# A state space scan followed by linear attention on one core: the state sums ahead of the next C row on TensorE, and D's products of a new y bank one slot sooner

## The chip, the cores and the metric

The kernel runs on one core of a Trainium2 chip. That core has five engines, each of which works through its own instructions in order: TensorE (PE in the profile; its weight loads are listed apart as PEld), VectorE (DVE), ScalarE (ACT), GpSimd (POOL), and SyncE (SP), which issues most of the transfers. The metric is the device time of one execution in microseconds (us). Before the change it was 7783.22 us, the median of three runs (7782.59 to 7801.19).

## The reference

The input is x, 4 x 512 x 64 x 64, in f32. Two layers are added to it, each on a group normalisation of what it gets.

The first is a state space model (Mamba). The 512 channels, normalised per token, are cut into four chunks of 128; each is a sequence of 4096 tokens. Per chunk:

```python
xz = einsum('bld,ed->ble', x, in_proj_w); xi, z = split(xz, 2)    # 256 inner channels each
xc = silu(conv(xi) + conv_b)                                      # 4 taps along the sequence
dt, Bs, Cs = x_proj(xc)                                           # Bs, Cs: 16 states
dt = softplus(dt_proj(dt) + dt_proj_b)
def step(h, inp):                                                 # for every token in turn
    dA = exp(dt_t[:, :, None] * A)
    h = dA * h + (dt_t * x_t)[:, :, None] * B_t[:, None, :]
    y = einsum('bds,bs->bd', h, C_t)                              # sum over the 16 states
y = (y + xc * D_param) * silu(z)
out = einsum('bld,od->blo', y, out_proj_w)
```

A skip, another normalisation over the 512 channels and a 512 x 512 projection follow. The second layer is linear attention with 8 heads: relu of q and k, k'q summed over all 4096 tokens of a batch, and v times that sum, normalised, with an output projection.

## The kernel before

**Tiles and steps.** The 4096 tokens of a batch are cut into 8 tiles of 512. One step works on one batch, tile and chunk, so there are 4 x 8 x 4 = 128 steps, four to a tile. The 256 inner channels are two halves `e` of 128. Four states and 32 channels lie on the 128 partitions, so a half needs four passes `q` over its 16 states, and a pass has four blocks `j` of 32 channels. A step thus has 8 passes and the kernel 1024.

**Slots.** The work is put down by hand, in slots (`slot`, L832 ff.). A pass has two slots, a step 16, numbered 0 to 15; `fold_states` of the pass in slots 0 and 1 is called in slot 2, and so on. In a slot:

- VectorE does two scans (L846) of 512 tokens, one for each block: `h = dA * h + bx`. The decay dA comes from ScalarE (L820) into one of three PSUM banks, bx from GpSimd (L828) into one of three buffers, two slots ahead.
- After the first scan of an even slot (the second in slot 10), `product` for the pass before: VectorE multiplies the first 384 columns of its h by the C row (L866). GpSimd has multiplied the last 128 columns by a part of C that came by DMA (L858, the tail product).
- Directly behind it `fold_states` gives TensorE its share of that pass, in the order below.
- `after()` then gives out everything else that falls to this slot: projections of the steps to come, normalisations, the output projection of the step before, and, from three queues (`ahead`, `late`, `rest`), pieces of the work between tiles. `rest` holds the attention of the batch before.

**What TensorE does in `fold_states`.** Three things, in this order:

1. The C row of the next pass (`c_row`): one bf16 product with a 0/1 matrix that spreads four rows of C over 128 partitions, 384 columns, into the one bank of `ps_c`. It overwrites the C row that `product` has just read, so it waits for `product`.
2. If the pass is the first of a half (`q == 0`, called in slots 2 and 10), a new y bank is taken from `ps_y`, which has one, and the diagonal goes into it: `D * xc` as four 32 x 32 products side by side (`diagonal`; 8 records in the profile, as each f32 product shows as two). The old y must have left the bank: ScalarE copies it out in `take_y` (L885), which is put down in slots 0 and 8.
3. The sum: four products with `fold`, side by side, that add the four states on the partitions (8 records). They read h, so they wait for `product` and for GpSimd's tail product.

h has two buffers. The first scan of a pass writes the buffer of two passes earlier, and needs that pass's sum to be done. After the fourth pass of a half, y is complete, and `take_y`, the gate and the output projection follow.

**How much goes into a slot.** TensorE's other work is rationed by a credit, in products of 512 columns. `mm` adds up what is given (`work["mm"]`); a diagonal counts 1.0, a sum 1.0, a C row 0.19. At the end of `after()`:

```python
credit = min(credit + 3.5 - (work["mm"] - seen), 2.6)
...                                    # pieces of ahead, late and rest, while credit > 0
seen = work["mm"]
```

So what `fold_states` gives between two calls of `after()` is charged at the next. Pieces of `rest` are given out only while the credit allows.

**After the loop** come the attention of the last batch and the output of its last tile, some 425 us with no scans.

All TensorE instructions are recorded by `mm`, so they share line L129 in the profile; they are told apart by tile: `c_all<-parts,sel` is the C row, `y<-xz,dg` the diagonal, `y<-h,fold` the sum.

Of the kernel before, what the change touches and what calls it, by code (L numbers as in the profile page):

```python
# [8 lines left out]
F32 = mybir.dt.float32  # L9
# [5 lines left out]
P = 128  # L15
T = 512
# [8 lines left out]
def kernel(  # L25
# [29 lines left out]
    NH = DI // P  # L55
# [14 lines left out]
    ps_y = ctx.enter_context(tc.tile_pool(name="ps_y", bufs=1, space=bass.MemoryType.PSUM))  # L70
# [55 lines left out]
    def mm(out_, lhsT, rhs, abreast=1, **how):  # L126

        work["mm"] += (0.25 if rhs.dtype == BF16 else 1.0) * rhs.shape[-1] / T / abreast
        nc.tensor.matmul(out_, lhsT, rhs, **how)  # L129
# [3 lines left out]
    def diagonal(out_, w, rhs):  # L133

        for k in range(P // BLK):
            r = slice(k * BLK, (k + 1) * BLK)
            mm(out_[r, :], w[r, :], rhs[r, :], abreast=P // BLK, start=True, stop=False)
# [130 lines left out]
    dg = const.tile([P, NH, BLK], F32, tag="dg", name="dg")  # L268
# [512 lines left out]
    SLOTS = NH * NQ * JJ  # L781
    AWAY = (3, 10)

    def place(g):

        n, r = divmod(g, SLOTS)
        e, r = divmod(r, NQ * JJ)
        return n, e, *divmod(r, JJ)

    b_all, c_all, c_sb, dAs, bxs, hs, ys = {}, {}, {}, {}, {}, {}, {}  # L790
# [18 lines left out]
    def c_row(g):  # L809
        n, e, q, _ = place(g)  # L810
        got = ps_c.tile([P, CUT], F32, tag="c", name=f"c_all_{g}")
        mm(got, sel[:, q, :], fs[n]["parts"], start=True, stop=True)
        c_all[g // JJ] = got
# [18 lines left out]
    def slot(g, last, after):  # L832
        n, e, q, jj = place(g)
        b, t, c = steps[n]
        if g + 2 < last:
            drive(g + 2)
        if jj == 0:
            if g + 3 * JJ < last:
                b_row(g + 3 * JJ)
            hs[g // JJ] = wk.tile([P, NJ, T], F32, tag="h", name=f"h_{g}", bufs=2)  # L840
        elif g + 1 < last:
            c_tail(g + 1)
        h = hs[g // JJ]
        for i in range(2):
            j = jj * 2 + i
            nc.vector.tensor_tensor_scan(  # L846
                h[:, j, :], dAs.pop(2 * g + i), bxs[g][:, i, :],
                0.0 if t == 0 else st[:, c, e, q, j : j + 1], ALU.mult, ALU.add,
            )
            if 2 * g + i + LEAD < 2 * last:  # L850
                decay(2 * g + i + LEAD)
            if i == int(g % SLOTS == AWAY[1]) and jj == 0 and g:
                product(g - 1)
                fold_states(g - 1, last)
        del bxs[g]
        if jj == JJ - 1:
            nc.gpsimd.tensor_copy(st[:, c, e, q, :], h[:, :, T - 1])  # L857
            nc.gpsimd.tensor_tensor(  # L858
                h[:, :, CUT:], h[:, :, CUT:], bc(c_sb.pop(g // JJ), NJ), ALU.mult
            )  # L860
        after()
# [6 lines left out]
    def fold_states(g, last):  # L868

        n, e, q, _ = place(g)  # L870
        if g + 1 < last:
            c_row(g + 1)
        if q == 0:
            ys[n, e] = ps_y.tile([P, T], F32, tag="y", name=f"y_{n}_{e}")
            diagonal(ys[n, e], dg[:, e, :], fs[n]["xz"][:, 0, e, :])
        h = hs.pop(g // JJ)
        for j in range(NJ):
            mm(
                ys[n, e][j * BLK : (j + 1) * BLK, :], fold, h[:, j, :],
                start=False, stop=(q == NQ - 1), abreast=NJ,  # L880
            )


    def take_y(f, n, e):
        nc.scalar.copy(f["xz"][:, 0, e, :], ys.pop((n, e)))  # L885
# [273 lines left out]
    fs = [{} for _ in steps]  # L1159
# [54 lines left out]
    def one(queue, may=ANYWHERE):  # L1214

        while queue:
            if queue[0][1] not in (None, "wait", "more", "free") and queue[0][1] not in may:
                return False  # L1220
            queue[0][1] = next(queue[0][0], queue)
            if queue[0][1] is not queue:
                return queue[0][1] != "wait"
            queue.pop(0)
        return False
# [67 lines left out]
    with tc.manual_schedule():  # L1293
        credit, seen, mix, held[0], held_x[0] = 0.0, work["mm"], iter(()), 0, 0
        for n, (b, t, c) in enumerate(steps):
            f, nm = fs[n], names[n]
# [9 lines left out]
            for s in range(SLOTS):  # L1306
                def after():
# [62 lines left out]
                    if s - 1 in AWAY:  # L1370
                        for queue in (ahead, late, rest):
                            if queue and queue[0][1] == "free":
                                one(queue)
                    seen = work["mm"]

                slot(n * SLOTS + s, N * SLOTS, after)
            fs[n - 1].clear() if n else None
        product(N * SLOTS - 1)
        fold_states(N * SLOTS - 1, N * SLOTS)
        now[0] = None  # L1380
        for _, what in due:
# [61 lines left out]
```

## Time and profile before

| | us |
|---|---|
| median of three runs | 7783.22 |
| the profiled execution, its own time | 7786.57 |
| its span, first to last instruction | 7784.8 |
| loop of the 128 steps, within the span | 92.8 to 7359.3 |
| C rows (1024): busy, mean of one | 367.5, 0.359 |
| diagonals (2048 records): busy, mean of one record | 354.9, 0.770 |
| sums (8192 records): busy, mean of one record | 1266.5, 0.694 |
| scans (3584 with a state): busy, mean of one | 4354.7, 1.264 |
| products (1024): busy, mean of one | 1767.7, 1.726 |
| tail products on GpSimd (1024): mean of one | 1.271 |
| bx on GpSimd (2048): busy, mean of one | 4826.9, 2.369 |
| TensorE idle ahead of a C row, until the product's end | 1004.0 in 462 places |

The mean granted clock of TensorE is 0.906. In the profile, busy times of an engine are unions: records that run side by side, like the four products of a sum, count once, so the mean of one record is not a fourth of the time of a sum. A wait is given with the instruction that waited and the one that ended the wait; only the last of several is named. In a row of the timeline the first number is the start, the second the length, and the bracket holds the idle time before it and what ended it.

### The profile page before, as it was taken

To read this page: it belongs to the slowest core of one execution; us is meant where nothing else is said; L and a number is where in the kernel's file an instruction comes from. 1 tells how busy PE (TensorE), PEld (TensorE's weight loads), DVE (VectorE), ACT (ScalarE), POOL (GpSimd) and SP (SyncE) were. 2 spreads that over 40 slices of the span, in tenths; PEclk is the share of its full clock that TensorE was granted. 3 is DMA by queue.
4 is the path that set the end of the run, shared out by engine and by line. 5 is a ranking of instruction groups with operands and counts; after the bars stand their busy time and mean duration, and the time that the engine had idled before them with its cause. 6 is when DMAs were issued, how large, how long until landed. Compare 5 with 4: busy or idle time off the path is not lost.

```text
span 7784.8 us, 90406 instructions
## 1 busy us (share of the span) xinstructions
PE 6430.9 (83%) x24784; PEld 2088.4 (27%) x24784; DVE 6983.2 (90%) x5816; ACT 5442.9 (70%) x8288; POOL 6897.0 (89%) x4638
## 2 busy tenths in 40 slices
PE   5677777767789888988789888898788888899699
PEld 1111221112223222322222223332122222233144
DVE  6999999999999999999999999899999999999821
ACT  5677777777777777777777777777777777777521
POOL 5999999999999999999999999999999999999700
PEclk8788788888899999998898999999799999999799
DMA  6666666666666656676766666677666655677502
GB/s 176 169 168 170 154 158 153 163 161 169 172 181 162 155 161 163 184 194 172 174 163 175 172 159 159 162 190 193 161 168 162 164 148 153 164 197 191 135 33 92
DMA packets 829216, 1265.33 MB, mean 163 GB/s; under 512 B 184072, under 2 KB 317720, under 8 KB 816416
## 3 DMA queue, kind: packets, MB, share of 16 engines
q1 hardware_dynamic: 806352, 1225.99, 60.3%
q0 software_dynamic: 16368, 32.51, 2.4%
q8 instruction: 194, 3.18, 0.2%
q14 instruction: 318, 2.61, 0.1%
q10 hardware_dynamic: 5984, 1.06, 0.1%
HBM read 1052.25 MB, written 206.57 MB: 162 GB/s over the span
## 4 chain that ended last, share of the span: by engine, by line
DVE 36%; PE 33%; ACT 10%; issue 7%; DMA 6%; POOL 5%; SPq 2%; DVEq 0%; POOLq 0%; ACTq 0%
DVE h L846 23%; DVE h L866 11%; PE y L129 6%; PE pc L129 6%; PE pq L129 6%; POOL bx L828 4%; ACT dA L820 4%; PE pr L129 3%; PE po L129 3%; PE pp L129 2%; DMA d_all<-d_rows 2%; DMA c_sb<-c_rows 2%; DVE xn L439 2%; SPq L795 2%; PE c_all L129 1%
## 5 line engine op out<-in xcount | busy, mean ns | idle before, releaser
L828 POOL TENSOR_TENSOR bx<-d_all,b_all 128x1024 f32<-128x1024 f32 x2048 | 4826.9, 2369 | 204.4 <-DVE h L846 187.5
L846 DVE TENSOR_TENSOR_SCAN h<-dA,st,bx 128x512 f32<-128x512 f32 x3584 | 4354.7, 1264 | 305.6 <-PE y L129 111.8
L820 ACT ACTIVATE dA<-d_all,a_t 128x512 f32<-128x512 f32 x4096 | 2759.0, 688 | 1499.1 <-DVE h L846 1445.2
L866 DVE TENSOR_TENSOR h<-h,c_all 128x1536 f32<-128x1536 f32 x1024 | 1767.7, 1726 | 0.1
L858 POOL TENSOR_TENSOR h<-h,c_sb 128x512 f32<-128x512 f32 x1024 | 1301.4, 1271 | 97.2 <-DMA c_sb<-c_rows 11.5
L129 PE MATMUL y<-h,fold 128*32 128x512 f32 x8192 | 1266.5, 694 | 51.6 <-POOL h L858 49.8
L129 PE MATMUL c_all<-parts,sel 128*128 128x384 bf16 x1024 | 367.5, 359 | 1005.5 <-DVE h L866 1004.0
L129 PE MATMUL pc<-xn,w_cv 128*128 128x512 f32 x2048 | 1047.6, 645 | 127.8 <-DVE xn L439 68.1
L129 PE MATMUL pq<-w_qk,xa 128*128 128x512 f32 x2048 | 965.9, 607 | 2.5 <-ACT xa L397 2.5
L846 DVE TENSOR_TENSOR_SCAN h<-dA,bx 128x512 f32<-128x512 f32 x512 | 590.0, 1202 | 39.1 <-POOL bx L828 15.5
L129 PEld LDWEIGHTS pc<-xn,w_cv 128*128 128x128 f32 x2048 | 389.9, 201 | 742.2 <-issue 413.5
L129 PEld LDWEIGHTS <-sel 128*128 128x128 bf16 x1216 | 120.6, 99 | 1655.6 <-DVE h L866 1443.1
L129 PEld LDWEIGHTS pq<-w_qk,xa 128*128 128x128 f32 x2048 | 394.1, 195 | 446.5 <-issue 429.1
L129 PE MATMUL pp<-xn,w_pr 128*128 128x512 f32 x1024 | 478.1, 596 | 0.0
L129 PE MATMUL pr<-xb,m 128*128 128x512 f32 x1024 | 475.6, 602 | 2.5 <-ACT res L1126 1.6
L129 PE MATMUL y<-xz,dg 32*32 32x512 f32 x2048 | 354.9, 770 | 0.0
L129 PEld LDWEIGHTS y<-h,fold 128*32 128x32 f32 x8192 | 170.4, 114 | 641.8 <-issue 393.4
L888 POOL TENSOR_TENSOR xz<-xz 128x512 f32<-128x512 f32 x256 | 325.7, 1272 | 12.1 <-ACT xz L885 9.7
L731 POOL TENSOR_TENSOR dt<-dt,xz 128x1024 f32<-128x1024 f32 x127 | 300.1, 2363 | 1.9 <-ACT dt L723 1.9
L129 PE MATMUL pd<-xz,w_xp 128*128 128x512 f32 x512 | 291.0, 696 | 0.0
L129 PE MATMUL pz<-xn,w_z 128*128 128x512 f32 x512 | 270.7, 621 | 7.8 <-ACT xz L710 6.3
L857 POOL COPY st<-h 128x4 f32<-128x4 f32 x1024 | 210.3, 205 | 59.0 <-DVE h L846 54.4
(223 smaller groups left out, 5911.7 us busy)
## 6 DMA issues: line engine op xcount, KB each, us to landing
d_all<-d_rows SPq DMA_DIRECT2D x2040, 256.0 KB, 4.3
b_all<-b_rows SPq DMA_DIRECT2D x4096, 64.0 KB, 2.4
d_rows<-dt SPq DMA_DIRECT2D x254, 512.0 KB, 2.7
c_sb<-c_rows SPq DMA_DIRECT2D x4096, 16.0 KB, 3.5
xn<-in_x_dram SPq DMA_DIRECT2D x32, 1024.0 KB, 8.0
x<-xr SPq DMA_DIRECT2D x32, 1024.0 KB, 4.4
xa<-x SPq DMA_DIRECT2D x32, 1024.0 KB, 5.7
xb<-x SPq DMA_DIRECT2D x32, 1024.0 KB, 5.8
```

Source lines behind the costliest of these rows:

```text
L129: nc.tensor.matmul(out_, lhsT, rhs, **how)
L439: nc.vector.tensor_tensor(v, v, bc(m, NC), op)
L731: nc.gpsimd.tensor_tensor(f["both"][:, 1], f["both"][:, 0], f["xz"][:, 0], ALU.mult)
L795: nc.sync.dma_start(dst[k * BLK : (k + 1) * BLK, :], rows_[q * KS + k, :].partition_broadcast(BLK))
L820: nc.scalar.activation(dAs[k], fs[n]["d_all", e][:, 0, j, :], AF.Exp, scale=a_t[:, e, j, q : q + 1])
L828: nc.gpsimd.tensor_tensor(bxs[g], fs[n]["d_all", e][:, 1, jj * 2 : jj * 2 + 2, :], bc(b_all[g // JJ], 2), ALU.mult)
L846: nc.vector.tensor_tensor_scan(h[:, j, :], dAs.pop(2 * g + i), bxs[g][:, i, :], 0.0 if t == 0 else st[:, c, e, q, j : j + 1], ALU.mult, AL ...
L857: nc.gpsimd.tensor_copy(st[:, c, e, q, :], h[:, :, T - 1])
L858: nc.gpsimd.tensor_tensor(h[:, :, CUT:], h[:, :, CUT:], bc(c_sb.pop(g // JJ), NJ), ALU.mult)
L866: nc.vector.tensor_tensor(own, own, bc(c_all.pop(g // JJ), NJ), ALU.mult)
L888: nc.gpsimd.tensor_tensor(f["xz"][:, 1, e, :], f["xz"][:, 1, e, :], f["xz"][:, 0, e, :], ALU.mult)
```

## The change

`fold_states` gives the sum first and the C row of the next pass behind it. Taking a new y bank and its diagonal become a function of their own, `begin_y`, called at the end of `after()` in slots 1 and 9: behind everything else of that slot on TensorE and just before `seen` is set. Before, the same happened in slots 2 and 10, between the C row and the sum.

```diff
     def fold_states(g, last):
 
         n, e, q, _ = place(g)
-        if g + 1 < last:
-            c_row(g + 1)
-        if q == 0:
-            ys[n, e] = ps_y.tile([P, T], F32, tag="y", name=f"y_{n}_{e}")
-            diagonal(ys[n, e], dg[:, e, :], fs[n]["xz"][:, 0, e, :])
         h = hs.pop(g // JJ)
         for j in range(NJ):
             mm(
                 ys[n, e][j * BLK : (j + 1) * BLK, :], fold, h[:, j, :],
                 start=False, stop=(q == NQ - 1), abreast=NJ,
             )
-
+        if g + 1 < last:
+            c_row(g + 1)
+
+
+    def begin_y(n, e):
+        ys[n, e] = ps_y.tile([P, T], F32, tag="y", name=f"y_{n}_{e}")
+        diagonal(ys[n, e], dg[:, e, :], fs[n]["xz"][:, 0, e, :])
...
                         for queue in (ahead, late, rest):
                             if queue and queue[0][1] == "free":
                                 one(queue)
+                    if s % (SLOTS // NH) == 1:
+                        begin_y(n, s // (SLOTS // NH))
                     seen = work["mm"]
```

## The prediction

> **What bounds the kernel now.** I read the busy times, the waits of VectorE, the chain, a table of stretches, and one piece of the timeline. The words pass, sum, C row and diagonal are those of the section on the kernel.
>
> ```profile
> PE 6430.9 (83%) x24784; PEld 2088.4 (27%) x24784; DVE 6983.2 (90%) x5816; ACT 5442.9 (70%) x8288; POOL 6897.0 (89%) x4638
> ...
> DVE 36%; PE 33%; ACT 10%; issue 7%; DMA 6%; POOL 5%; SPq 2%; DVEq 0%; POOLq 0%; ACTq 0%
> ```
>
> No engine is alone in front. The stretches (length; busy time and instructions of PE, PEld, DVE, ACT, POOL; granted clock; DMA) show it for the loop and, in its order, for three tiles of the loop:
>
> ```profile
> 92.80:7359.30 7266.50, 5976.30 (x23246) 1882.48 (x23244) 6846.85 (x5514) 5329.61 (x8122) 6884.89 (x4617) 0.90 0.66 168
> ...
> 3235.70:3461.60 225.90, 202.58 (x737) 67.14 (x736) 212.46 (x165) 171.90 (x263) 215.21 (x144) 0.97 0.74 195
> 3461.60:3686.60 225.00, 188.00 (x690) 58.64 (x688) 211.60 (x164) 168.52 (x257) 214.17 (x144) 0.93 0.68 179
> 3686.60:3904.60 218.00, 161.47 (x603) 44.35 (x603) 209.34 (x181) 162.61 (x248) 214.89 (x150) 0.83 0.71 178
> ```
>
> In the loop VectorE is busy 94.2% and GpSimd 94.7%. VectorE's idle time there is 420 us, and its waits (waiter, releaser: us, times, longest) say what a reorder on TensorE can reach:
>
> ```profile
> DVE h L846 <- PE y L129: 126.7, 119, 3.7
> DVE h L846 <- ACT dA L820: 94.9, 101, 3.5
> ...
> DVE h L846 <- POOL bx L828: 51.2, 51, 5.5
> ```
>
> Counting scans in order (32 a step) puts the 126.7 us in slots 4 (14.3), 6 (18.3), 8 (25.1), 10 (17.8), 12 (43.5) and 14 (7.6): always the first scan of a pass, which needs the h buffer that the sum of two passes earlier frees. Slots 4 and 12, 57.8 us in 56 waits, follow the first pass of a y bank. One of them:
>
> ```profile
> 1394.78 1.73 DVE L866 TENSOR_TENSOR h<-h,c_all 128x1536 f32<-128x1536 f32 x1
> 1394.89 0.69 ACT L820 ACTIVATE dA<-d_all,a_t 128x512 f32<-128x512 f32 x1 [0.48 <-DVE h L846]
> ...
> 1396.42 2.45 DVE L846 TENSOR_TENSOR_SCAN h<-dA,st,bx 128x512 f32<-128x512 f32 x2
> ...
> 1396.56 0.50 PE L129 MATMUL c_all<-parts,sel 128*128 128x384 bf16 x1 [3.72 <-DVE h L866]
> ...
> 1396.99 1.93 PE L129 MATMUL y<-xz,dg 32*32 32x512 f32 x8
> ...
> 1398.85 1.50 PE L129 MATMUL y<-h,fold 128*32 128x512 f32 x8
> ...
> 1400.60 1.28 DVE L846 TENSOR_TENSOR_SCAN h<-dA,st,bx 128x512 f32<-128x512 f32 x1 [1.73 <-PE y L129]
> ```
>
> TensorE idles 3.72 us for the product, then does C row and diagonal, 2.3 us that the freed buffer does not need, and only then the sum; VectorE waits 1.73 us. In all 119 waits the scan starts 0.2 us after the sum's end.
>
> **The change part by part.** No instruction is added or removed. On TensorE the C row goes behind the sum in all 1024 passes, and the diagonal, 8 records, goes to the end of the slot before in 256. Neither has a DMA, and nothing moves past a queue of SyncE or GpSimd by itself.
>
> *Sum ahead of C row.* From the C row's start to the sum's start takes 0.26 us (median, passes without diagonal). In the 63 waits outside slots 4 and 12 (69.0 us), I set the sum's new start at the latest of product's end, GpSimd's tail product's end and TensorE's previous work, and let no scan start before its dA and bx are there: 11.4 us go. 63 x 0.26 would be 16 us; some sums wait for GpSimd anyway, and most of these waits have TensorE behind by more than a C row.
>
> *C row later.* The next product needs it. From the sum's end to that product's start the trace has at least 1.30 us in every pass (one scan lies between), and a C row takes 0.36 us, 0.50 at most at half clock: cost 0. Were the scan not there, each pass would lose up to 0.36 us, 368 us in all. The sum now carries the wait for the product as well as that for the tail product, so the C row and what is behind it also stand behind a late tail (50 us in 55 waits); the trace already has the sum waiting there, and the next user, the product, has the 1.30 us.
>
> *Diagonal earlier.* The 256 diagonals take 355 us from first start to last end, 1.39 each. A new one must wait for ScalarE's copy of the old y bank (L885); that ends at least 2.0 us, in the median 3.6 us, before the product's end. Between the later of that copy and TensorE's previous work, and the product's end, the diagonal fits wholly in 163 cases, in part in 24, not at all in 69: 269 of 355 us go into idle time. Behind the diagonal on TensorE stand only the sum and the C row, which wait for the product anyway. By the same rule as above, 32.7 of the 57.8 us in slots 4 and 12 go; the rest has TensorE behind.
>
> *TensorE's lead.* What it gains in a first pass is carried to the next sum as far as it does not idle between: 5.8 us more. Direct sum: 11.4 + 32.7 + 5.8 = 49.9 us.
>
> *What is late next.* After 27 of the 119 waits (25.9 of 126.7 us, 20%) VectorE's next wait is for GpSimd or ScalarE, which had not themselves waited for VectorE since; there the gain is lost. 80% of 49.9 is 40. The chain runs through 51 of the waits, and 26.8 of the 49.9 us lie there: the lower bound. The upper: the chain holds 88 diagonals with 101 us that would fit into idle time; with 51 x 0.26 for the C rows, 114. I take 38, the middle of 27 and 50, for the waits are the nearer row: a chain that loses a part is replaced by another soon.
>
> *The credit.* The loop gives other TensorE work to a slot by a credit of 3.5 products, less what was given since the last count. The new call stands just before that count, so the diagonal, 1 product, is no longer charged, twice a step. In the order of the built programs the attention of a batch ends 12 or 13 passes earlier: 34 products leave the tile at 3461.60 for the four or five before it, 34 in the second batch, 22 in the third: 90 x 0.94 us (965.9 us for 1024 products of pq) = 85 us of TensorE time in denser places. Lower bound: the emptied tiles come down towards the 218.0 us of one without attention, about 6 us each, 17 us gained. Upper bound: the denser places are as long as TensorE's work, 85 - 17 = 68 us lost. The stretches above are nearer to nothing: 14.6 us more TensorE time costs 0.9 us. I take 0. The attention's loads and stores on SyncE's queue move forward with it, in their own order; the DMA engines are busy 66% in the loop, and I put nothing on them beyond these bounds.
>
> Sum against the profiled execution (7786.57 us, span 7784.8): 7786.6 - 38 = 7748.6. The median of the runs is 3.3 us lower: **7745 us**, 0.5% faster. A measurement of this kernel tells about 0.3% (23 us) from no change.
>
> **The clock.** In the timeline above the C row takes 0.50 and the diagonal 1.93 us, against 0.33 and 1.06 at full clock; 117 of the 256 sums of first passes are that long. C row, diagonal and sum are now one run of some 4 us behind the wait; afterwards they are two of about half of that. TensorE: Matmul & The Clock Gate of the Trainium skill (Part 1) says that half clock is the default, that some 3.4 us of sustained activity release it and that an idle window of that length brings it back. By that rule the split could leave TensorE at half clock, or the diagonal in the gap could keep it awake; no run here shows which.
>
> **The rivals.**
> - *GpSimd takes the place.* It is busier than VectorE in the loop, and its waits for VectorE (187.5 us for bx buffers) are what it could give. Against it: the chain has it at 5% only. It would keep a quarter of the 49.9 us: 7771.
> - *Clock lost.* If the other 139 sums run at half clock too, 0.87 us each, 121 us of TensorE time return. The sums of first passes still end earlier (they start 1.23 us earlier on average), but half the direct gain goes and the work behind is later: 7763. This is the mechanism of the Trainium skill's page on the clock gate, taken against the change.
> - *Denser attention, slower.* Place: the tiles from 2300.9 to 3461.6 and their like in later batches. Price 68 us, against 38 gained: 7813. It decides from 0.61 us of time per moved product ((38 + 17) / 90). For it: two tiles of the query stage, 201.98 us of TensorE time in 230.90 and 209.85 in 237.00, give 0.8 us per us. Against: the lines above, 0.06.
> - *The chain is right.* All of the chain's diagonals that fit go: 7669.
> - That the change does not do what it says: the order of the built program shows each diagonal and C row at its new place; under 1%, counted with no change.
>
> **Chances.** Forecast 0.50, GpSimd 0.17, clock 0.08, denser attention 0.13, chain 0.12. The range leaves out the slower case (0.13) and half of the chain's (0.06): 7690 to 7800. The forecast's own range, from the 27 us of the chain's waits to 65 gained (between the 50 and the 114), is 7718 to 7756. Faster by over 0.3% (below 7760): 0.46 of the forecast, 0.12 of the chain's, 0.03 of GpSimd's: 0.61. Slower (above 7806): 0.12. Within: 0.27.
>
> **What would show it.** VectorE's wait for PE y falls from 126.7 to about 77 us, in slots 4 and 12 from 57.8 to about 25. TensorE's wait for the product stands before the sum, not before the C row, and falls from 1004 by up to 269 us. No product waits for a C row. The tiles with attention keep their length, and the one at 3461.60 shortens. I am wrong if waits for bx or dA grow by what PE y loses, if the tiles with queries grow by more than 5 us each, or if the granted clock (0.906) falls.

## The result and the profile after

The changed kernel takes 7736.03 us, median of six runs (7731.83 to 7750.91), against 7782.91 for six runs of the kernel before on the same chip. The ratio is 0.9940, with a 95% interval of 0.9927 to 0.9954: 47 us, or 0.6%, faster. A later set of five runs gave 7738.0, ratio 0.9949 (0.9936 to 0.9961). The profiled execution took 7737.52 us, with a span of 7735.7.

The busy times and the chain by engine, from the page after:

```profile
PE 6406.8 (83%) x24758; PEld 2126.6 (27%) x24784; DVE 6982.3 (90%) x5816; ACT 5441.6 (70%) x8288; POOL 6890.0 (89%) x4638
...
PE 30%; DVE 25%; ACT 12%; DMA 11%; issue 9%; POOL 8%; SPq 4%; DVEq 0%; POOLq 0%; ACTq 0%
```

No engine does noticeably less work. VectorE is busy as long as before, so the gain is idle time of VectorE. The stretches after (length; busy time and instructions of PE, PEld, DVE, ACT, POOL; granted clock; DMA) are the loop, eight tiles without attention, the attention of the first batch, and three tiles one by one: the last two of that attention and the tile behind it:

```profile
93.20:7308.80 7215.60, 5947.50 (x23212) 1920.76 (x23236) 6846.95 (x5513) 5328.84 (x8123) 6877.40 (x4617) 0.90 0.66 169
...
307.40:2065.50 1758.10, 1296.82 (x4764) 365.89 (x4765) 1706.45 (x1362) 1288.54 (x1948) 1716.83 (x1153) 0.81 0.66 164
...
2065.50:3668.60 1603.10, 1404.91 (x5599) 479.54 (x5605) 1512.38 (x1223) 1199.39 (x1836) 1508.28 (x1012) 0.94 0.67 172
...
3218.50:3447.10 228.60, 208.24 (x753) 70.48 (x751) 212.47 (x164) 172.40 (x264) 210.18 (x140) 0.96 0.74 196
3447.10:3668.60 221.50, 173.70 (x626) 51.39 (x626) 211.86 (x164) 163.92 (x249) 213.25 (x144) 0.82 0.65 165
3668.60:3888.20 219.60, 159.34 (x602) 46.26 (x603) 210.02 (x180) 162.40 (x247) 216.41 (x150) 0.84 0.70 177
```

The loop went from 7266.5 to 7215.6 us (-50.9); VectorE's busy time in it went from 6846.85 to 6846.95. The two stretches of the kernel before that answer to the second and third line were:

```profile
310.10:2069.90 1759.80, 1281.22 (x4765) 344.94 (x4765) 1705.29 (x1363) 1286.77 (x1948) 1718.37 (x1153) 0.83 0.66 164
2069.90:3686.60 1616.70, 1420.08 (x5605) 476.49 (x5605) 1513.34 (x1223) 1199.36 (x1836) 1510.85 (x1012) 0.94 0.66 171
```

The eight tiles without attention gained 1.7 us, and their TensorE time rose by 15.6 us at a lower clock. The attention of the first batch alone gained 13.6 us. Over the whole loop, 11 tiles without attention went from 2413.3 to 2411.5 us, and 21 with it from 4853.2 to 4804.1. So nearly all the gain is in tiles with attention.

The waits of VectorE after (waiter, releaser: us, times, longest):

```profile
DVE h L846 <- PE y L129: 145.7, 114, 6.6
DVE h L846 <- ACT dA L820: 83.8, 113, 2.8
...
DVE h L846 <- POOL bx L828: 50.9, 64, 1.8
...
DVE kq L962 <- PE pk L129: 18.0, 20, 4.0
```

By this row the wait for a sum, which the change is about, did not fall: it was 126.7. But the row is not the whole wait. The first scan of a pass needs three things from other engines in time: the h buffer that a sum frees, its dA and its bx. In the kernel before, 97 more waits of such scans, 114.9 us, are named for other instructions, though the scan's own dA and bx had been ready for 0.4 us or more (in the median 2.4). These scans start as long after the sum's end as the 119 do, 0.17 or 0.23 us in nearly all; where dA or bx ends a wait, it is 0.03 us. One of them, named for a copy that the scan does not read, while the sum ended 0.17 us ahead of it:

```profile
2448.97 1.06 PE L129 MATMUL y<-h,fold 128*32 128x512 f32 x8
2449.50 0.58 ACT L899 COPY xn<-po 128x512 f32<-128x512 f32 x1
...
2450.20 1.28 DVE L846 TENSOR_TENSOR_SCAN h<-dA,st,bx 128x512 f32<-128x512 f32 x1 [2.69 <-ACT xn L899]
```

Below, "by end times" means that a scan's wait is counted for whichever of sum, dA and bx ended last. By end times the wait for a sum fell from 241.6 us (216 waits) to 195.6 (168), that for bx grew from 27.0 to 48.2, and that for dA from 72.7 to 82.9.

Here is where VectorE's idle time in the loop went, 419.6 to 368.6 us in all, by the instruction that follows it: ahead of scans 344.7 to 329.6 (-15.1), ahead of the sums of kq, where the attention's weight product is taken over, 49.1 to 16.6 (-32.5), ahead of the output of the attention 16.2 to 8.7 (-7.5). The sums of kq wait for TensorE's product pk; that wait stood before at

```profile
DVE kq L961 <- PE pk L129: 49.8, 35, 3.6
```

The waits for a sum by end times, put into their slots by counting the scans:

| slot | 0 | 4 | 6 | 8 | 10 | 12 | 14 |
|---|---|---|---|---|---|---|---|
| before, us | 0.2 | 15.8 | 37.0 | 79.0 | 17.8 | 83.7 | 8.0 |
| after, us | 16.7 | 0 | 28.7 | 99.6 | 16.8 | 30.7 | 3.2 |

Slots 4 and 12 fall from 99.6 to 30.7 us; slots 0 and 8 take 37 us back.

### The profile page after: what moved, and what is told of

Same layout as the page of the kernel before. It is cut to its first block, busy times and chain, and to the rows that moved or that the text cites. A ratio compares the mean times of both kernels' runs of the same rounds, so it can differ in the third digit from the quotient of the medians.

```text
span 7735.7 us, 92385 instructions
## 1 busy us (share of the span) xinstructions
PE 6406.8 (83%) x24758; PEld 2126.6 (27%) x24784; DVE 6982.3 (90%) x5816; ACT 5441.6 (70%) x8288; POOL 6890.0 (89%) x4638
## 3 DMA queue, kind: packets, MB, share of 16 engines
q10 hardware_dynamic: 5984, 1.06, 0.1%
## 4 chain that ended last, share of the span: by engine, by line
PE 30%; DVE 25%; ACT 12%; DMA 11%; issue 9%; POOL 8%; SPq 4%; DVEq 0%; POOLq 0%; ACTq 0%
DVE h L846 15%; DVE h L866 8%; PE pc L129 7%; POOL bx L828 5%; ACT dA L820 5%; PE pq L129 5%; PE y L129 4%; DMA d_all<-d_rows 4%; PE pr L129 3%; PE pp L129 3%; SPq L795 3%; PE po L129 3%; DMA c_sb<-c_rows 2%; DVE xn L439 2%; DMA b_all<-b_rows 2%
## 5 line engine op out<-in xcount | busy, mean ns | idle before, releaser
L129 PE MATMUL y<-h,fold 128*32 128x512 f32 x8192 | 1295.1, 682 | 874.2 <-DVE h L866 507.9
L129 PE MATMUL pc<-xn,w_cv 128*128 128x512 f32 x2048 | 1099.2, 672 | 195.8 <-DVE xn L439 130.4
L129 PEld LDWEIGHTS y<-h,fold 128*32 128x32 f32 x8192 | 206.8, 114 | 1715.3 <-POOL h L858 838.3
L129 PEld LDWEIGHTS pc<-xn,w_cv 128*128 128x128 f32 x2048 | 411.3, 210 | 744.8 <-issue 415.6
L129 PE MATMUL y<-xz,dg 32*32 32x512 f32 x2048 | 316.6, 690 | 43.0 <-ACT xz L886 42.8
L889 POOL TENSOR_TENSOR xz<-xz 128x512 f32<-128x512 f32 x256 | 325.9, 1273 | 10.6 <-ACT xz L886 10.3
L129 PE MATMUL pd<-xz,w_xp 128*128 128x512 f32 x512 | 275.1, 665 | 0.0
L129 PEld LDWEIGHTS pr<-xb,m 128*128 128x128 f32 x1024 | 196.5, 196 | 275.0 <-issue 227.7
```

The lines of the kernel that those rows point to most:

```text
L889: nc.gpsimd.tensor_tensor(f["xz"][:, 1, e, :], f["xz"][:, 1, e, :], f["xz"][:, 0, e, :], ALU.mult)
```

## The experiments

Every run stands beside runs of the kernel before on the same chip (median 7782.8, 7782.1 and 7780.5 us in three sets). The first theory was that of the prediction: the time gained is VectorE's wait for sums, shortened by the two moves on TensorE. Its rivals after the first look at the traces were the credit, since by the named rows the wait that fell is that of the sums of kq; GpSimd, since the tiles without attention kept their length; and the clock. "Charged" means that the credit counts the diagonal, as before; "uncharged" that it does not, as after the change. Idle times by slot, half-clock records and the ends of sums are counted from the instructions in the traces.

### One part at a time: charged, credit_only, sum_first, diag_only

The changed kernel with the diagonal charged again:

```diff
+                    seen = work["mm"]
                     if s % (SLOTS // NH) == 1:
                         begin_y(n, s // (SLOTS // NH))
-                    seen = work["mm"]
```

> The whole change, but the early diagonal is given just behind the count of the credit, so that it is charged to slots 2 and 10 as before; VectorE, ScalarE and GpSimd then get their work in the old order. Order theory (the prediction's: the sums come earlier, the credit is worth nothing): about 45 us faster than before, 7737, as the changed kernel. Credit theory (VectorE's idle time ahead of scans fell by only 15 us from before to after, that ahead of the kq sums by 32, so most of the gain is the other place of the attention's pieces): 10 to 15 us faster, 7768 to 7773, with the wait of kq for pk back at about 50 us.

Measured: 7762.53 us, ratio 0.9978 (0.9969 to 0.9987). The reorder alone is worth 20 us; the missing charge is worth the other 25 to 27 (7736.03 and 7738.0 are the changed kernel's two medians).

The kernel before with only the charge taken away:

```diff
             diagonal(ys[n, e], dg[:, e, :], fs[n]["xz"][:, 0, e, :])
+            work["mm"] -= 1.0
```

> The kernel before with one thing changed: a diagonal is no longer counted in the credit. Its order within a pass is the old one (C row, diagonal, sum). Order theory: no change, 7775 to 7790. Credit theory: 25 to 35 us faster, 7748 to 7758, with kq's wait for pk near 18 us and the waits for PE y not below 126.7 us.

Measured: 7772.11 us, ratio 0.9985 (0.9976 to 0.9994). The idle time ahead of the sums of kq fell from 49 to 24.5 us, that ahead of scans rose from 344.7 to 358.3: -25 and +14, net -11.

The kernel before with only the C row moved behind the sum; the diagonal stays in `fold_states`, ahead of the sum:

```diff
-        if g + 1 < last:
-            c_row(g + 1)
         if q == 0:
             ...
         for j in range(NJ):
             ...
+        if g + 1 < last:
+            c_row(g + 1)
```

> Only the sum ahead of the C row; the diagonal stays in slots 2 and 10 ahead of the sum, and is charged. Order theory, from the prediction's terms: 11.4 us of direct waits plus 0.26 us in each of the 56 waits of slots 4 and 12, 26 us in all, of which 80% pass: 20 us faster, 7763. Credit theory: up to 5 us faster, no more than that.

Measured: 7762.98 us, ratio 0.9977 (0.9968 to 0.9986), the same as `charged`. That is no chance. In the built programs the two have the same order of instructions on all five engines, and so have `sum_first` with an uncharged diagonal and the changed kernel. With the C row gone from its front, the diagonal has no instruction between its old place and its new one that waits for the product: "one slot sooner" moves nothing, and the diagonal goes by the first edit already into the gap, the idle time of TensorE until the product's end. The change is two edits: sum and diagonal ahead of the C row, and a diagonal that is not charged. The 7763 expected from the prediction's terms was met, but the runs below split these 20 us into two parts of opposite sign, a loss and a larger gain.

The changed kernel with the C row back ahead of the sum: the diagonal alone is early, and uncharged.

```diff
         h = hs.pop(g // JJ)
+        if g + 1 < last:
+            c_row(g + 1)
         for j in range(NJ):
             ...
-        if g + 1 < last:
-            c_row(g + 1)
```

> Only the diagonal one slot sooner, not charged, with the C row still ahead of the sum. Order theory: what is left of the gain without the 20 us of the C row, 25 to 30 us faster, 7753 to 7758. Credit theory: the credit's 25 to 35 us and a little for the diagonal, 35 to 45 us faster, 7738 to 7748.

Measured: 7781.12 us, ratio 0.9999 (0.9990 to 1.0008). The diagonal in the gap, which the prediction gave most of the gain, brings nothing even with the credit; both theories had expected a gain.

### The size of the credit: after_again, same_total, more_credit, sum_3625

The changed kernel once more, with no edit, as the measure for this set.

> The changed kernel as it is, on the chip and beside the runs of the next three. The sum ahead of the C row alone gave 20 us, the credit alone 11. If the two only add up: 31 us faster, 7752. If the first measurement holds: 47 us faster, 7736, and 16 us come from having both.

Measured: 7738.0 us, ratio 0.9949 (0.9936 to 0.9961).

The changed kernel with the two uncharged products taken back evenly, 16 x 0.125 = 2 a step:

```diff
-                    credit = min(credit + 3.5 - (work["mm"] - seen), 2.6)
+                    credit = min(credit + 3.375 - (work["mm"] - seen), 2.6)
```

> The changed kernel with a credit of 3.375 a slot in place of 3.5: the two products a step that are no longer charged are taken back evenly, so the attention has the old amount and only the place of the extra products (slots 2 and 10) differs. Theory amount (a denser attention is over sooner): the credit's part goes, 20 us faster than before, 7763, as with the sum alone. Theory place (the pk products come to lie where their sums do not hold VectorE up): the gain stays at 40 us or more, 7743 or less, with kq's wait for pk near 18 us.

Measured: 7771.17 us, ratio 0.9984 (0.9975 to 0.9993). The wait ahead of the sums of kq is back (53.6 us), and the attention of the batches ends at passes 503, 759 and 1001, against 483, 739 and 994. The profiled execution is the fastest of its eleven (7754.91), so its waits stand for the quick end. Neither theory is met: with about the old amount, the place in slots 2 and 10 alone gains nothing over `charged` (7762.53).

The changed kernel with a larger credit:

```diff
-                    credit = min(credit + 3.5 - (work["mm"] - seen), 2.6)
+                    credit = min(credit + 3.75 - (work["mm"] - seen), 2.6)
```

> The changed kernel with a credit of 3.75 a slot. Theory amount: the attention ends some 20 passes earlier again, and 10 to 25 us more are gained, 7715 to 7726. Theory place: no order in it, within 15 us of the changed kernel either way. Should TensorE be the bound in the tiles with attention (it is busy 87 to 92% there after the change), the waits for PE y grow and the time rises.

Measured: 7843.12 us, ratio 1.0083 (1.0069 to 1.0097), 61 us slower than before. By end times the scans wait 248.4 us for a sum, 77.1 for bx and 90.2 for dA, against 195.6, 48.2 and 82.9 after the change.

Attention ends still earlier (473, 729, 977), and now the idle time ahead of scans is 419.4 us, against 329.6. The prediction's slower rival, denser attention, is real; it begins at a larger credit than the change gives.

`sum_first` with 2 products a step more, as many as the missing charge gives, but spread over all 16 slots:

```diff
-                    credit = min(credit + 3.5 - (work["mm"] - seen), 2.6)
+                    credit = min(credit + 3.625 - (work["mm"] - seen), 2.6)
```

> The sum ahead of the C row with the diagonal charged, and a credit of 3.625 a slot: the same amount of credit a step as the changed kernel, spread over all slots; the attention of the first two batches ends in the same pass as there (483 and 739). Theory amount: as the changed kernel, 7731 to 7743. Theory place: another time, 7755 or more, and with it another wait of kq for pk than 18 us or other waits ahead of the scans.

Measured: 7760.98 us, ratio 0.9976 (0.9966 to 0.9985). The attention ends at passes 483 and 739 as in the changed kernel, the wait ahead of the sums of kq is as short (18.4 us), and yet nothing is gained over `sum_first`: the idle time ahead of scans is 347.9 us. So the amount alone does not pay, and by `same_total` neither does the place alone. But this run is not a clean test of the place. In the tiles without attention the changed kernel has the same order on TensorE as `sum_first`; here the larger credit changes it, 19 places of 598 in one such tile. Those 11 tiles are 8 us longer than in `sum_first`, and their scans in slot 10 wait 17.3 us for a sum by end times, against 0.6. The tiles with attention are 9 us shorter than in `sum_first`; in the changed kernel they are 25 us shorter. What is left for the place is the 16 us between these two.

### The diagonal's place: diag_charged, sum_c_diag, sum_c_diag_credit

`diag_only` with the diagonal charged, so that against the kernel before only the diagonal's place on TensorE differs:

```diff
+                    seen = work["mm"]
                     if s % (SLOTS // NH) == 1:
                         begin_y(n, s // (SLOTS // NH))
-                    seen = work["mm"]
```

> Only the diagonal one slot sooner, charged in the old slots, with the C row still ahead of the sum: all other work keeps its old order. Prediction's terms: 32.7 us of direct waits in slots 4 and 12 (less the 0.26 us in each that belong to the C row), of which 80% pass: 15 to 25 us faster, 7758 to 7768. From the run with the diagonal alone and not charged, which was no faster: 7775 to 7785.

Measured: 7809.25 us, ratio 1.0040 (1.0027 to 1.0052): 27 us slower. Its waits of VectorE:

```profile
DVE h L846 <- ACT dA L820: 99.8, 116, 3.5
DVE h L846 <- PE y L129: 89.0, 81, 4.2
...
DVE h L846 <- POOL bx L828: 55.0, 63, 5.5
DVE h L846 <- ACT xn L900: 38.0, 30, 3.0
...
DVE h L846 <- POOL st L857: 27.3, 26, 1.8
```

By its row the wait for a sum fell by 37.7 us, but most of the waits named xn and st here are for a sum as well. By end times it fell by 17.8 us, from 241.6 to 223.8: slots 4 and 12 from 99.6 to 47.6, while slots 6 and 8 rose from 116.0 to 156.4. The wait for bx grew from 27.0 to 51.5. In tiles without attention the idle time ahead of scans shows the exchange: slot 4 falls from 12 to 2 us and slot 12 from 33 to 12, slot 8 rises from 23 to 47, of which 25.1 are for a sum and 22.0 for bx. The stretch of the eight tiles:

```profile
308.10:2075.60 1767.50, 1324.02 (x4764) 359.65 (x4765) 1708.32 (x1362) 1287.28 (x1948) 1718.24 (x1153) 0.81 0.67 163
```

It has 42.8 us more TensorE time than before, at a clock of 0.81 against 0.83, for the same instructions.

The opposite: the sum first, then the C row, and the diagonal last, so that the gap holds nothing and TensorE's work stands in one run behind the wait. The sum opens the bank, the diagonal adds to it.

```diff
-    def diagonal(out_, w, rhs):
+    def diagonal(out_, w, rhs, first=True):
...
-            mm(out_[r, :], w[r, :], rhs[r, :], abreast=P // BLK, start=True, stop=False)
+            mm(out_[r, :], w[r, :], rhs[r, :], abreast=P // BLK, start=first, stop=False)
...
+        if q == 0:
+            ys[n, e] = ps_y.tile([P, T], F32, tag="y", name=f"y_{n}_{e}")
...
-                start=False, stop=(q == NQ - 1), abreast=NJ,
+                start=(q == 0), stop=(q == NQ - 1), abreast=NJ,
...
         if g + 1 < last:
             c_row(g + 1)
+        if q == 0:
+            diagonal(ys[n, e], dg[:, e, :], fs[n]["xz"][:, 0, e, :], False)
```

> The order sum, C row, diagonal: the sum opens the new y bank and the diagonal is added to it behind the C row, in slots 2 and 10, charged as before. The sum comes as early as with the sum alone ahead of the C row, but the diagonal leaves TensorE's idle time ahead of the product and lies behind it again. Theory gap (the diagonal in the idle time is what cost 27 us where the C row stayed in front): 20 to 30 us faster than with the sum first, 7733 to 7743. Theory lead (work in idle time is a gain, the prediction's): the 1.2 us a first pass return behind the sum, 5 to 15 us slower than with the sum first, 7768 to 7778.

Measured: 7729.94 us, ratio 0.9934 (0.9922 to 0.9947): 33 us faster than `sum_first`, which has the diagonal in the gap and the same charge. Theory lead is refuted, and the time is just below the range of theory gap. But the run changes more than the gap: the sum no longer stands behind a diagonal either, where TensorE comes too late to have done the diagonal in the gap. By end times the wait for a sum falls from 174.9 us to 120.1, and 36.6 of that in slots 4 and 12 (39.0 to 2.4). The stretch of the eight tiles:

```profile
312.30:2057.80 1745.50, 1266.01 (x4765) 355.71 (x4765) 1706.16 (x1362) 1286.75 (x1949) 1715.50 (x1153) 0.82 0.68 165
```

58 us of TensorE time less than with the diagonal in the gap and the C row first (1324.0), and 30.8 less than after the change (1296.8), for the same work. Next, the group of the convolution's products, none of which was touched (busy, mean ns of one record, then the idle time ahead and what ended it). In the kernel before:

```profile
L129 PE MATMUL pc<-xn,w_cv 128*128 128x512 f32 x2048 | 1047.6, 645 | 127.8 <-DVE xn L439 68.1 <-ACT xz L693 28.0 <-ACT dt L723 18.8
```

In `diag_charged`:

```profile
L129 PE MATMUL pc<-xn,w_cv 128*128 128x512 f32 x2048 | 1107.0, 676 | 205.8 <-DVE xn L439 140.5 <-ACT dt L723 34.0 <-ACT xz L693 18.3
```

In the changed kernel:

```profile
L129 PE MATMUL pc<-xn,w_cv 128*128 128x512 f32 x2048 | 1099.2, 672 | 195.8 <-DVE xn L439 130.4 <-ACT dt L723 32.0 <-ACT xz L693 16.8
```

In `sum_c_diag`:

```profile
L129 PE MATMUL pc<-xn,w_cv 128*128 128x512 f32 x2048 | 1040.1, 642 | 97.9 <-DVE xn L439 52.1 <-ACT xz L693 18.4 <-ACT dt L723 16.0
```

One record is longer wherever the diagonal stands in the gap. The count is sharper. Records over 0.9 us had a granted clock of 0.50 to 0.53 on average, those up to 0.7 us one of 1.00. Of the 2048 records, those over 0.9 us are 169 before, 113 with the credit only and 172 with the diagonal last; with the diagonal in the gap (`diag_only`, `diag_charged`, `sum_first`, `charged` and the changed kernel) they are 286 to 320. Of the 44 sums of a step's second pass (called in slot 4) in the tiles without attention, 1, 1 and 2 are at half clock in the first three; 15 to 21 in the five. The mean granted clock of slot 4 in these tiles says the same: 0.96 before and 0.81 in `sum_c_diag`, but 0.64 in `diag_charged`, 0.57 in `sum_first` and 0.55 in the changed kernel; in slots 6 to 9 it is 0.95 or more in all five. What that looks like is in TensorE's timeline of one and the same step, picked as an example, since the state differs from step to step and the counts carry the reading (start, length, what; in the bracket the idle time ahead and what ended it). The kernel before:

```profile
1587.25 0.50 PE L129 MATMUL c_all<-parts,sel 128*128 128x384 bf16 x1 [3.56 <-DVE h L866]
1587.69 1.93 PE L129 MATMUL y<-xz,dg 32*32 32x512 f32 x8
1589.54 1.72 PE L129 MATMUL y<-h,fold 128*32 128x512 f32 x8
...
1592.26 1.99 PE L129 MATMUL pc<-xn,w_cv 128*128 128x512 f32 x4
...
1594.69 1.06 PE L129 MATMUL y<-h,fold 128*32 128x512 f32 x8
```

The changed kernel:

```profile
1580.46 1.93 PE L129 MATMUL y<-xz,dg 32*32 32x512 f32 x8
1584.19 1.94 PE L129 MATMUL y<-h,fold 128*32 128x512 f32 x8 [1.80 <-DVE h L866]
...
1588.50 3.78 PE L129 MATMUL pc<-xn,w_cv 128*128 128x512 f32 x4
1592.21 1.49 PE L129 MATMUL y<-h,fold 128*32 128x512 f32 x8
```

And `sum_c_diag`:

```profile
1577.74 1.93 PE L129 MATMUL y<-h,fold 128*32 128x512 f32 x8 [3.68 <-DVE h L866]
...
1580.03 1.93 PE L129 MATMUL y<-xz,dg 32*32 32x512 f32 x8
...
1583.04 1.99 PE L129 MATMUL pc<-xn,w_cv 128*128 128x512 f32 x4
1584.96 1.07 PE L129 MATMUL y<-h,fold 128*32 128x512 f32 x8
```

Before and in `sum_c_diag`, some 4 us of work behind the wait run at half clock (the diagonal takes 1.93 us, not 1.06), and the convolution's products are back at full clock, 1.99 us for four records. After the change the diagonal is 1.8 us ahead of the rest, and the convolution's products still run at half clock 4 us behind the wait: 3.78 us. The Trainium skill's page TensorE: Matmul & The Clock Gate (Part 1) says that half clock is the default and that some 3.4 us of sustained activity release it. By the granted clock in the traces the release came 3.7 us behind the wait in the kernel before and 4.4 us in `sum_c_diag`, which agrees with that. In the changed kernel it came 8.9 us behind the wait, though TensorE worked without a break; why it takes that long there is open. In tiles without attention the sum of a step's third pass (called in slot 6) then ends 4.0 us behind its product on average, against 3.0 before and 3.5 in `sum_c_diag`. The first scan of slot 8 needs it: by end times that is 24.4 us of slot 8's 46.1 after the change, against 10.3 of 22.6 before, and nearly all the rest is for bx.

The same order with the charge taken away:

```diff
             diagonal(ys[n, e], dg[:, e, :], fs[n]["xz"][:, 0, e, :], False)
+            work["mm"] -= 1.0
```

> The same order, with the diagonal not charged: the changed kernel with its diagonal put back behind the product. Theory gap: faster than the changed kernel, 7710 to 7720. Theory lead: slower than it, 7741 to 7755.

Measured: 7723.57 us, ratio 0.9929 (0.9915 to 0.9942). It has the lowest median of all the runs, 12 us under the changed kernel; against `sum_c_diag` it is not told apart, since the intervals overlap.

### Is it GpSimd in the tiles without attention? nogate_sum

GpSimd is busy 97.8% of the tiles without attention (2359.1 of 2413.3 us before), so it could be what keeps their length. `sum_first` without the gate product:

```diff
-        nc.gpsimd.tensor_tensor(
-            f["xz"][:, 1, e, :], f["xz"][:, 1, e, :], f["xz"][:, 0, e, :], ALU.mult
-        )
+        pass
```

> The sum ahead of the C row, without the gate: the product of y with silu(z) on GpSimd (L888, 1.27 us, twice a step) is left out, so z does not enter the result. Theory GpSimd bound (in the 11 tiles without attention GpSimd is busy 98% of the time, and these tiles did not shorten with the sum first): each of them shortens by most of the 10.2 us that its eight gates take, from 219 to 211 to 214 us, where VectorE's 211.6 us of work hold it. Theory TensorE bound: they stay at 217 to 219.

Measured: 7725.16 us, ratio 0.9929 (0.9915 to 0.9942), 38 us less than `sum_first`. The eight tiles in `sum_first`:

```profile
309.60:2067.30 1757.70, 1298.06 (x4765) 366.36 (x4765) 1706.36 (x1362) 1288.43 (x1948) 1716.70 (x1153) 0.81 0.68 164
```

Without the gate product:

```profile
306.80:2043.20 1736.40, 1294.85 (x4765) 367.56 (x4765) 1703.64 (x1362) 1287.83 (x1948) 1645.43 (x1089) 0.81 0.69 166
```

GpSimd's work falls by 71.3 us, the stretch by 21.3: 30% of what a bound would give. Over the 11 tiles without attention it is 3.0 us a tile (2412.6 to 2379.2). In these, the wait for bx in slot 8 falls from 21.6 us to 2.9 by end times. (The output projection no longer waits for the gate either, 7.0 us on TensorE in `sum_first`.) GpSimd is part of what holds these tiles, not the whole. The order on TensorE is another part: `sum_c_diag` brings the 11 tiles to 2402.8, at a clock of 0.825 against 0.806, with all of GpSimd's work.

### The runs together

| order on TensorE in a half's first pass | charged | uncharged |
|---|---|---|
| wait, C row, diagonal, sum | 7782 (before) | 7772 |
| diagonal, wait, C row, sum | 7809 | 7781 |
| diagonal, wait, sum, C row | 7763 | 7736, 7738 (changed) |
| wait, sum, C row, diagonal | 7730 | 7724 |

In the other passes the C row leads in the first two rows and the sum in the last two. Read down a column: sum ahead of the C row with the diagonal in the gap is -46 charged and -43 to -45 uncharged; diagonal into the gap with the C row first is +27 and +9; out of the gap with the sum first is -33 and -12 to -14. So the reorder is worth the same with and without the charge, and the diagonal's place is not. Read across, the missing charge is -25 to -28 where the diagonal is in the gap and -6 to -11 where it is not. Each of these differences is uncertain by some 10 us. The changed kernel, by this table: +27 for the diagonal, -46 for the sum, -26 for the charge. These are three steps of one way through the table, so that they add up to its gain is no test of them.

The waits of scans by end times, and all idle time ahead of scans, in the profiled executions (us):

| kernel | for a sum | for bx | for dA | idle ahead of scans |
|---|---|---|---|---|
| before | 241.6 | 27.0 | 72.7 | 344.7 |
| `diag_charged` | 223.8 | 51.5 | 76.5 | 356.1 |
| `sum_first` | 174.9 | 65.3 | 80.6 | 323.8 |
| `sum_c_diag` | 120.1 | 53.6 | 113.7 | 291.1 |
| `credit_only` | 241.0 | 34.3 | 78.7 | 358.3 |
| `diag_only` | 228.3 | 52.8 | 75.3 | 360.8 |
| changed | 195.6 | 48.2 | 82.9 | 329.6 |
| `sum_c_diag_credit` | 140.5 | 46.1 | 111.4 | 300.6 |

Each step of the order, as the first four rows and the last four have it, shortens the wait for a sum. Part of it comes back as a wait for bx or dA; at the step that puts the diagonal into the gap with the C row first, more than all of it.

## Why the prediction was right, and where not

The sign, the range and nearly the size were right: 38 us were taken, 47 came. But the total held because its terms erred in opposite directions, and in that the size is luck.

- **Diagonal earlier: wrong in sign.** The step that failed is "269 of 355 us go into idle time", with 32.7 us of waits gone. The direct part came, and more: in `diag_charged` the waits for a sum in slots 4 and 12 fall by 52.0 us by end times. But the work behind was taken to keep its durations. With the diagonal gone from the run behind the wait, the convolution's products and the next sums stay at half clock for longer; 40.4 us come back as waits for a sum in slots 6 and 8, and 24.5 as waits for bx: +27 us charged, +9 uncharged. How much of that the clock makes is open (last section). The working had the rows, C row 0.50 us against 0.33 and diagonal 1.93 against 1.06, and put them in a rival with a chance of 0.08; it sized that rival by the sums of first passes, and of those 47 of 256 run at half clock after the change, against 117: they lost nothing. The long records lie behind them, in the convolution's products and the second pass, and the third pass's sum ends later for it.
- **Sum ahead of the C row: undersized.** 11.4 us direct was the price by 63 waits, 69.0 us, outside slots 4 and 12. The row of 126.7 us held only the waits that the profile names for a sum; by end times there are 124 outside these slots, 142.1 us. In the runs the reorder is worth about 46 us where the diagonal's place is the same in both kernels, and between these two (`diag_charged` and `sum_first`) the wait for a sum falls by 48.9 us. No run has this reorder with the diagonal left between the wait and the sum: without the C row ahead of it, the diagonal goes into the gap.
- **C row later costs nothing: right.** No product waits: VectorE's longest idle time ahead of one is 0.1 us, before and after.
- **TensorE's wait moves from the C row to the sum: right.** The waits of TensorE after:

```profile
PE y L129 <- DVE h L866: 507.9, 266, 5.6
PE y L129 <- POOL h L858: 310.0, 129, 5.8
```

  and the C row's, before:

```profile
PE c_all L129 <- DVE h L866: 1004.0, 462, 6.4
```

  The sum waits for product and tail product, so GpSimd is now named for part of it. All idle time ahead of the sums in the loop is 873 us, against 1004 ahead of the C rows and 51 ahead of the sums before: 182 less, within the "up to 269" foreseen.
- **The credit at 0: wrong.** With the sum first it is 25 to 27 of the 47 us. The step named both bounds, 17 gained and 68 lost, and took 0 by the stretch at 3235.70. The lower bound's part came: the last tiles of the three batches' attention are 10 us shorter than in `charged` (16.5 than before, where 17 was named). The rest is what neither bound was about: the sums of kq wait less for pk (49.1 to 16.6 us). `sum_3625` moves the attention as far and gains nothing in all, because the scans wait more; `same_total`, with the place but not the amount, gives the gain back. Why both are needed is open. One reading is that the products fill the run from which the diagonal was taken, since the charge matters most where the diagonal is in the gap (25 to 28 us, against 6 to 11); but the convolution's records are no shorter for it (676 and 674 ns in `diag_charged` and `diag_only`), so the clock does not show it.
- **What is late next: undersized.** By end times the wait for a sum fell by 46.0 us, near the direct 49.9, but the waits for bx and dA grew by 31.4: two thirds came back, where a fifth was taken. In `charged`, without the credit, 65.5 us fell (241.6 to 176.1) and 44.3 came back, and 20 us were measured. Tiles without attention gained 1.8 us in 2413; GpSimd explains 30% by `nogate_sum`, the order on TensorE another part by `sum_c_diag`.
- **Signs.** The row of waits for PE y was to fall to 77 and is 145.7; by end times the wait for a sum fell by 46.0. That waits for bx and dA grow by what it loses was named as a sign of being wrong: the rows do not show it, by end times two thirds of it happened. Tiles with attention were to keep their length and lost 49 us in 4853, where nearly all the gain is. The last tile of the first batch's attention did shorten, 225.0 to 221.5, and the tile ahead of it grew by 2.7, less than the 5 named as the limit. The granted clock fell, 0.906 to 0.900, which was named as a sign of being wrong: it did tell of a loss, and the loss was covered by the two gains that were priced too low.

## What to carry to other kernels

Price a move on an in-order engine by what it does to the engine's clock behind the move as well as to the waits ahead of it: a short piece of work put into an idle gap, and so taken out of the run behind the wait, cost more here than it saved, with a lower granted clock behind it. Let the work that others wait for go first behind the wait and let the rest follow in the same run: sum, C row, diagonal was the best order of the four. Before pricing a row of waits, compare its names with the ends of what the waiting instruction needs: here nearly half of the wait for a sum stood under other names. And when an edit also moves a count that rations other work, make the two separately before believing either: here the ration was more than half of the gain and was nowhere in the edit's description.

## What the runs showed of the hardware that was not expected

A gap of idle time on TensorE is not free room. With the same instructions, moving 256 diagonals of 1.39 us into the gap ahead of a wait raised TensorE's busy time in the eight tiles without attention from 1281.2 to 1324.0 us (`diag_charged`) and lowered the granted clock of the tiles without attention from 0.825 to 0.808; putting them behind the sum and the C row gave 1266.0 us and 0.825. TensorE's idle time ahead of the convolution's products, waiting for their input xn, follows the same split: 68.1 and 52.1 us with the diagonal behind the wait, 140.5 and 130.4 with it in the gap. By these rows TensorE comes there sooner and then waits. Whether this rest or the cut ahead of the sum is what keeps the clock low, the runs don't tell apart. Nor do they show that the clock makes the whole loss: of `diag_charged`'s 20 us in the profiled loop, 12.4 lie in the tiles without attention, where the clock fell, and 7.3 in those with it, where it is 0.939 against 0.940. Still less does it make the whole gain of `sum_c_diag` over `sum_first`: of 35 us in the profiled loop, 9.8 lie in the tiles without attention and 25.3 in those with it, where the clock is 0.941 in both. There the waits for a sum in slots 4 and 12 fall from 32.7 us to 2.1 by end times, which putting the sum ahead of the diagonal can give without the clock.

In every trace here the granted clock is either full or half, and each stretch of one or the other, but for those at the ends of the trace, lasts a whole multiple of 3.41 us.
